# One shared gather for six rarely used neighbour slots, removed-edge cells fetched once at the end, and a payload move cut in four, in a four-layer graph kernel on one core

## The chip, the cores and the metric

The kernel runs on one core of a Trainium2 chip. A core has five engines that work side by side, each with its own queue of instructions in a fixed order: PE (matrix products), DVE (vector work), ACT (scalar functions and copies), POOL (here mostly the issue of indirect DMAs, that is gathers) and SyncE (SP, which issues plain DMAs). The metric is the device time of one execution in microseconds. Ten executions of the kernel before gave a median of 1512.22 us, from 1508.64 to 1516.35.

## The reference

Sixteen independent graphs of 1024 nodes with 64 features go through four layers. Each layer normalises the nodes, takes the positive part, does something with the adjacency matrix (0 or 1, about four neighbours per node, not symmetric) and adds the result to x. Layers 0, 1 and 3 are dense products with the adjacency matrix. Layer 2 is the one that matters here:

```python
# --- layer 2 (adj_preln) ---
h = jnp.maximum(_layernorm(x, axis=-1), 0.0)
adj_ = jnp.where(eye[None], 1.0, adj)
nb = (adj_ > 0) & (~eye)[None]              # neighbours without oneself
m = nb.sum(-1)
rank = jnp.cumsum(nb, axis=-1) - 1
skip = jnp.where(m > 10, (m + 1) // 2, 1)   # nodes of more than 10 neighbours lose some
do_dil = (skip > 1) & mask
removed = nb & do_dil[..., None] & ((rank + 1) % skip[..., None] == 0)
rem = removed | jnp.swapaxes(removed, 1, 2) # an edge is removed both ways
adj_d = jnp.where(rem, 0.0, adj_)
# per node and feature: the neighbours' h sorted, and a weighted sum of their
# quartiles (0.25, 0.5, 0.25), interpolated between ranks
agg = _weighted_nanquantile_agg(h, adj_d > 0)
y = relu((h + agg) @ W1 + b1) @ W2 + b2
x = x + y * mask[..., None]
```

So each node's few neighbours (with itself) have to be fetched as rows of h and sorted per feature.

## The kernel before

**Pairs and phases.** The graphs are worked on in eight pairs (`fast`, line 1794). For each pair, `first` loads the adjacency rows (`fast_graph`, line 1087: one 512 KB transfer of 128 rows on SyncE's queue, transposed on PE, copied by ACT, counted by ACT, the positions of the first eight neighbours found by DVE), orders the nodes by degree (`by_degree`, line 1111), makes neighbour lists (`dilated`, line 1202) and computes layers 0 and 1 and the normed input of layer 2, which goes to a table in DRAM (`fast_to_table`, line 1558). `second` gathers and sorts (`fast_quantiles`, line 1367), brings the sums back into the order of the nodes (`unsorted`, line 1467) and computes the rest of layers 2 and 3 (`fast_to_output`, line 1629). `first` of the next pair stands in the program before `second` of this one, so the two overlap.

**Sorting by degree.** The 1024 nodes of each graph are cut into 16 pieces of 64 nodes of falling degree; the two graphs of a pair lie side by side on the 128 partitions. A piece has room for only as many neighbours as its largest node needs: `CAPS = (15, 7, 6, 6, 5, 5, 5, 4, 4, 4, 3, 3, 3, 2, 2, 1)`. The lists are moved into this order by a product with one-hot matrices; for it, one DVE instruction (line 1174, `moved`) multiplies each node's payload of 11 numbers with its one-hot piece, 128 x 2816 elements.

**Lists.** The piece of the largest nodes has 16 slots: 15 for neighbours and one for the node itself. The positions of the neighbours beyond eight are found in the nodes' own adjacency rows, which POOL fetches with one gather (`high`, line 1212), then DVE runs some thirty small instructions that end in the indices `idx`, the cells of removed edges `where`, and the weights. For each pair POOL fetches from DRAM the cells that lie opposite to removed edges (`hits`, lines 1275 to 1287; two gathers). They are given a due time that is 150 us later (`LATE`).

**Gathers.** Each slot of each piece is one gather of 128 rows of 64 floats (line 1323): 75 neighbour slots and 16 own slots, so 91 per pair. The slots lie in three tiles: piece 0 (16 slots), pieces 1 to 6 (8 slots each) and pieces 7 to 15 (5 slots each). DVE sorts the three one after the other with min and max networks (`compared`, line 1328), with one scratch tile `side`.

**Buffers.** The matmul outputs of the phases have buffers of their own: `prod` and `node`, one each for the first graph's layers, the second graph's layers, and `second` (phase `_b`). All products of `second`, among them layer 3's, take turns in its single `prod`.

**The order of the work.** Nothing is issued as it is written. `Plan` (line 243) notes every instruction with a cost and a landing time from `cost` (line 380), and a due time `want` (66 us per graph, `PERIOD`). `order` (line 309) then plays the engines through: at each step an engine takes, of the instructions whose inputs are ready in the plan, the one whose due time less the longest path behind it is least. That fixes the queue of each engine; on the chip each engine waits at the head of its queue.

**The check at the end.** `checked` (line 1846) compares counts with what the lists held, and marks in `bad` and `over` the pairs for which the lists were not enough; a removed edge whose opposite cell is set also marks its pair. `redo` (line 1042) sums the marks on PE (`any_node`, line 973), and a loop of a general, slow version runs for marked graphs only. These instructions come after the plan, and their places in the queues are found by the framework: `seen` and `bad` run at 1276 to 1277 us, the last of `bad` at 1400.33 us, the sum on PE at 1400.90 us. In the time shown the loop has no turn.

## Time and profile before

| | |
|---|---|
| median of ten executions | 1512.22 us |
| profiled execution: time, span | 1510.82 us, 1509.0 us |
| busy: PE, DVE, ACT, POOL | 1054.1, 954.3, 740.6, 812.2 us |
| gathers of neighbours: count, mean | 600, 1064 ns |
| gathers of the nodes themselves: count, mean | 128, 1089 ns |
| gathers of cells (`hits`): count, mean | 16, 1035 ns |
| payload move: count, duration | 8, 3083 ns |
| TensorE clock granted, mean | 0.866 of full |

A line of the profile names the engine, the operation, the tile it writes, the tiles it reads, shapes, and how often; in an order of time the first number is the start from the beginning of the span, the second the time it took, and the brackets hold how long the engine stood idle before it and what ended that. Nearly all instructions are issued from one line of the program (369), so a step is told by its tiles: `slots` are the gathered rows, `side` the sorts' scratch, `high` the fetched adjacency rows, `prod` and `node` matmul outputs, `rest` and `low` the parts of a product's operand, `u`, `x`, `h` node features, `back` one-hot matrices. For a SyncE issue the time in an order of time that is merged runs over several, their waits included.

### The profile page before, as it was taken

The page shows a single profiled execution, that of the slowest core. Times are in us where ns is not written, and L with a number is a line of the kernel's source. Part 1 is how long each engine was busy: PE and PEld are TensorE (multiplying, and loading weights), DVE is VectorE, ACT ScalarE, POOL GpSimd, SP SyncE. Part 2 cuts the span into 40 slices and gives each one's busy share as a digit, 9 for nine tenths or more (in the row PEclk, how much of TensorE's full clock was granted, in tenths as well). Part 3 has the DMA queues.
Part 4 walks back from the last instruction along what each step waited for, and adds up shares of the span by engine and source line. Part 5 has one row for each costly group of instructions (what it writes and reads, how often), then busy time and mean ns, then how long its engine had stood idle before and what let it go on. Part 6 is the DMA issues. An engine that isn't in the chain of part 4 may idle for free.

```text
span 1509.0 us, 26159 instructions
## 1 busy us (share of the span) xinstructions
PE 1054.1 (70%) x9898; PEld 649.9 (43%) x9898; DVE 954.3 (63%) x2375; ACT 740.6 (49%) x2010; POOL 812.2 (54%) x771
## 2 busy tenths in 40 slices
PE   1588696739876879688867886797868974620266
PEld 1355463415554455445643554455544542210132
DVE  7536574877578839675868756966687467510841
ACT  1947846733565575645574557556653531210012
POOL 2000277827772778267845776277717772777000
PEclk9989797869998999899989998998989997755577
DMA  4604413512252333222343234223411111111000
GB/s 124 206 3 135 125 24 106 156 46 39 54 156 55 90 84 101 89 71 53 98 127 79 47 86 150 71 42 93 115 52 32 32 31 27 25 33 26 10 1 17
DMA packets 96111, 109.98 MB, mean 73 GB/s; under 512 B 66792, under 2 KB 66920, under 8 KB 95976
## 3 DMA queue, kind: packets, MB, share of 16 engines
q1 hardware_dynamic: 36840, 71.66, 14.9%
q0 software_dynamic: 24960, 28.11, 10.2%
q10 hardware_dynamic: 34176, 8.46, 2.6%
q8 instruction: 79, 1.29, 0.4%
q14 instruction: 56, 0.46, 0.1%
HBM read 99.77 MB, written 8.39 MB: 72 GB/s over the span
## 4 chain that ended last, share of the span: by engine, by line
POOL 51%; issue 20%; DVE 12%; PE 10%; DMA 4%; ACT 3%; SPq 0%; ACTq 0%; DVEq 0%; POOLq 0%
POOL slots L369 51%; PE prod L369 7%; DVE slots L369 3%; DVE side L369 3%; PE node L369 2%; ACT u L369 2%; DMA high<-in_adj_dram,at_row 1%; DMA slots<-table,self_idx 1%; DVE found L369 1%; ACT junk L369 1%; DMA row<-in_adj_dram 1%; DVE agg_low L369 1%; DVE more L369 1%; DVE past L369 0%; DMA slots<-table,idx 0%
## 5 line engine op out<-in xcount | busy, mean ns | idle before, releaser
L369 POOL DMA_INDIRECT slots<-table,idx x600 | 638.3, 1064 | 381.2 <-issue 208.7
L369 PE MATMUL prod<-at,rest 128*64 128x512 fp8e4 x1280 | 220.5, 413 | 90.3 <-DVE rest L369 87.3
L369 PE MATMUL prod<-at,low 128*64 128x512 fp8e4 x1280 | 218.8, 408 | 12.4 <-DVE low L369 12.0
L369 PE MATMUL prod<-at,u 128*64 128x512 fp8e4 x1280 | 218.2, 408 | 8.4 <-ACT u L369 8.0
L369 DVE TENSOR_TENSOR side<-slots 128x384 f32<-128x384 f32 (+6 forms) x160 | 92.3, 616 | 187.9 <-DMA slots<-table,self_idx 156.6
L369 ACT ACTIVATE u<-node,d 128x64 f32<-128x64 f32 x640 | 140.6, 333 | 76.2 <-PE node L369 75.7
L369 PEld LDWEIGHTS <-rest 128*64 128x64 bf16 x1792 | 99.1, 117 | 171.8 <-DVE rest L369 104.3
L369 ACT COPY rest<-prod 128x512 f32<-128x512 f32 x80 | 47.2, 591 | 256.5 <-PE prod L369 234.3
L369 ACT ACTIVATE junk<-row,unit 128x1024 fp8e4<-128x1024 f32 x128 | 150.1, 1172 | 41.7 <-DMA row<-in_adj_dram 40.8
L369 POOL DMA_INDIRECT slots<-table,self_idx x128 | 139.4, 1089 | 39.0 <-issue 38.4
L369 DVE FIND_INDEX8 found<-ones,row 128x8 uint32<-128x1032 f32 x128 | 156.5, 1224 | 0.0
L369 ACT ACTIVATE at<-tr 128x1024 fp8e4<-128x1024 bf16 x128 | 132.1, 1055 | 48.5 <-PE tr L369 30.1
L369 ACT ACTIVATE u<-x,off,by 128x64 f32<-128x64 f32 x384 | 133.8, 438 | 22.5 <-DVE off L369 18.5
L369 PEld LDWEIGHTS <-u 128*64 128x64 bf16 x1792 | 100.9, 117 | 98.7 <-issue 28.1
L369 PEld LDWEIGHTS <-low 128*64 128x64 bf16 x1792 | 99.0, 116 | 92.0 <-DVE low L369 23.2
L369 PE MATMUL tr<-ident_bf,row 128*128 128x128 bf16 x1024 | 84.5, 238 | 52.8 <-ACT at L369 52.5
L369 PE MATMUL prod<-back,side 64*64 64x512 bf16 x256 | 54.7, 402 | 77.8 <-DVE side L369 77.8
L369 PEld LDWEIGHTS <-row 128*128 128x128 bf16 x1024 | 70.6, 107 | 69.5 <-issue 65.3
L369 PE MATMUL node<-wbd,ft_sb 128*128 128x128 f32 x512 | 96.9, 290 | 4.0 <-ACT ft_sb L369 4.0
L369 DVE TENSOR_TENSOR rest<-u 128x512 f32<-128x512 f32 x80 | 54.8, 689 | 63.5 <-ACT u L369 62.9
L369 PE MATMUL node<-ident,rest 128*128 128x128 f32 x384 | 81.3, 295 | 15.2 <-ACT rest L369 15.1
L369 PEld LDWEIGHTS node<-wbd,ft_sb 128*128 128x128 f32 x512 | 78.6, 204 | 6.9 <-ACT ft_sb L369 5.0
(228 smaller groups left out, 1958.4 us busy)
## 6 DMA issues: line engine op xcount, KB each, us to landing
row<-in_adj_dram SPq DMA_DIRECT2D x128, 512.0 KB
slots<-table,idx POOLq DMA_INDIRECT x600
x<-in_x_dram ACTq DMA_DIRECT2D x32, 128.0 KB
table<-h SPq DMA_DIRECT2D x32, 128.0 KB
out_dram<-u ACTq DMA_DIRECT2D x32, 128.0 KB
slots<-table,self_idx POOLq DMA_INDIRECT x128
hits<-in_adj_dram,where POOLq DMA_INDIRECT x16
wd<-in_L_gnn_W_dram SPq DMA_DIRECT2D x2, 64.0 KB
```

Of the source, the lines that this page charges most:

```text
L369: f(*[real(x) for x in s.args], **{k: real(x) for k, x in s.kw.items()})
```

## The change

Six slots of piece 0, those for the tenth to the fifteenth neighbour, are used by few of its 64 nodes, and by the ones of highest degree, which lie first. `SHARED` gives each of these slots a number of leading nodes: 24, 12, 8, 8, 6, 6, together 64. Their indices are put below one another in one index column `rare`, by twelve small SyncE transfers from `idx` (one per slot and half); one gather fetches these 128 rows into `got`; PE moves them to their places with one matrix of shifts per slot, on top of a product that fills the places of the other nodes with a large number, and ACT copies the result into the slots (`shared`). The check of capacities now knows the number of nodes per slot.

The cells of removed edges are no longer fetched per pair. The first 16 nodes of each half write their cell numbers and flags to a common tile `cells` (two small SyncE transfers and an ACT copy per pair), and `strike`, which is noted ahead of the last pair's `second`, fetches them all with four gathers and multiplies them with the flags into `struck`. `bad` no longer reads fetched cells: it takes the flags of nodes beyond the first 16 alone; `struck` is summed on PE with two further matmuls for each half.

The payload move is issued as four instructions of a quarter each. `past` shares a buffer with `there`. The planner's costs are new on all engines, and every instruction notes a stage name, which nothing reads here.

```diff
+SHARED = ((9, 24), (10, 12), (11, 8), (12, 8), (13, 6), (14, 6))
+NEAR = SHARED[0][0]
+FIRST = 16
@@ cost
-        return 1.3, 1.7 if out.shape[-1] < N else 3.5
+        return 1.33, 1.7 if out.shape[-1] < N else 3.5
...
-            return (0.065 if narrow else 0.145), 0.2
+            return (0.067 if narrow else 0.115), 0.2
         if any(x.dtype in NARROW for x in wide):
-            return max(0.06, n * 0.25e-3), 0.25
-        return max(0.1, n * 1.15e-3), 0.25
+            return max(0.03, n * 0.213e-3), 0.25
+        return max(0.06, n * 0.9e-3), 0.25
     if engine == "scalar":
-        more = 0.19 if kw.get("accum_out") is not None else 0.0
-        return 0.19 + 0.84e-3 * n + more, 0.06
+        more = 0.2 if kw.get("accum_out") is not None else 0.0
+        for x in ("scale", "bias"):
+            more += 0.1 if isinstance(kw.get(x), Noted) else 0.0
+        return 0.18 + 0.84e-3 * n + more, 0.06
@@ sorted_constants
+        for n, (k, w) in enumerate(SHARED):
+            nc.vector.tensor_scalar(held, place, float(w), None, ALU.is_lt)
+            nc.vector.tensor_tensor(self.caps[:, 0:1], self.caps[:, 0:1], held, ALU.add)
...
+            nc.vector.memset(self.shifts[:, n, :], 0.0)
...
@@ by_degree
-        nc.vector.tensor_tensor(
-            moved,
-            pay.unsqueeze(2).to_broadcast([P, 2 * T, S, PAY]),
-            tile_hot.unsqueeze(3).to_broadcast([P, 2 * T, S, PAY]),
-            ALU.mult,
-        )
+        for a in range(0, 2 * T, HT):
+            shape = [P, HT, S, PAY]
+            nc.vector.tensor_tensor(
+                moved[:, a : a + HT],
+                pay[:, a : a + HT].unsqueeze(2).to_broadcast(shape),
+                tile_hot[:, a : a + HT].unsqueeze(3).to_broadcast(shape),
+                ALU.mult,
+            )
@@ dilated
-        self.plan.want += LATE
-        for n in range(2):
-            nc.gpsimd.indirect_dma_start(
-                out=self.hits[pair][:, n : n + 1],
...
-        self.plan.want -= LATE
+        nc.scalar.copy(cell[:, 2:4], gone)
+        for i in range(2):
+            nc.sync.dma_start(
+                out=self.cells[pair * FIRST : (pair + 1) * FIRST, i, :],
+                in_=cell[i * HP : i * HP + FIRST, :],
+            )
...
+        rare = self.p_lists.tile([P, 1], U32, name="rare")
+        off = 0
+        for k, w in SHARED:
+            for i in range(2):
+                a = i * HP
+                nc.sync.dma_start(
+                    out=rare[a + off : a + off + w, :], in_=idx[a : a + w, k // E, k % E : k % E + 1]
+                )
+            off += w
@@ new
+    def shared(self, out, table, index):
+        nc = self.nc
+        got = self.p_sort.tile([P, F], F32, name="got", bufs=1)
+        self.gather(got, table, index)
+        n = len(SHARED)
+        ps = self.ps_prod.tile([P, n, F], F32, name="rare", tag="prod")
+        nc.tensor.matmul(
+            ps,
+            lhsT=self.ident,
+            rhs=self.absent.unsqueeze(2).to_broadcast([P, n, F]),
+            start=True,
+            stop=False,
+        )
+        for k in range(n):
+            nc.tensor.matmul(
+                ps[:, k, :], lhsT=self.shifts[:, k, :], rhs=got, start=False, stop=k == n - 1
+            )
+        nc.scalar.copy(out, ps)
@@ fast_quantiles
-                for k in range(cap):
+                for k in range(NEAR if s == 0 else cap):
                     self.gather(slots[:, s - lo, k, :], table, own[:, k : k + 1])
+                if s == 0:
+                    self.shared(slots[:, 0, NEAR:cap, :], table, rare)
                 self.gather(slots[:, s - lo, cap, :], table, self_idx[:, s : s + 1])
@@ fast
             if pair + 1 < len(pairs):
                 first(pair + 1)
+            else:
+                self.strike()
             second(pair)
@@ new
+    def strike(self):
+        nc = self.nc
+        where = self.p_lists.tile([P, 2, 2], U32, name="where", bufs=1)
+        nc.vector.tensor_copy(where, self.cells[:, :, 0:2])
+        hits = self.p_lists.tile([P, 2, 2], F32, name="hits", bufs=1)
+        nc.gpsimd.memset(hits, 0.0)
...
+        for i in range(2):
+            for n in range(2):
+                nc.gpsimd.indirect_dma_start(
+                    out=hits[:, i, n : n + 1],
...
+        nc.vector.tensor_tensor(self.struck, hits, self.cells[:, :, 2:4], ALU.mult)
@@ checked
-            nc.vector.tensor_tensor(bad[:, :, S : S + 2], hits, gone, ALU.mult)
+            nc.vector.tensor_scalar(bad[:, :, S : S + 2], gone, self.spare, None, ALU.mult)
@@ redo
                 flags = self.any_node(
-                    pool, self.ps_tr, f"batches{i}", self.over, self.halves[:, i : i + 1]
+                    pool,
+                    self.ps_tr,
+                    f"batches{i}",
+                    self.over,
+                    self.halves[:, i : i + 1],
+                    [(self.struck[:, i, n : n + 1], self.pair_rows) for n in range(2)],
                 )
```

## The prediction

> **What bounds the kernel now.** I read the page's busy shares and its chain first, then the stretches cut at the ends of POOL's gather runs, then POOL, DVE and SyncE in order of time.
>
> ```profile
> PE 1054.1 (70%) x9898; PEld 649.9 (43%) x9898; DVE 954.3 (63%) x2375; ACT 740.6 (49%) x2010; POOL 812.2 (54%) x771
> POOL 51%; issue 20%; DVE 12%; PE 10%; DMA 4%; ACT 3%; SPq 0%; ACTq 0%; DVEq 0%; POOLq 0%
> ```
>
> PE is busiest, but the chain that ends last is POOL's: 51%, and most of the 20% "issue" is the 0.30 us between two gathers. The averages hide two alternating stretches, here for pair 2 (start and end; then PE, PEld, DVE, ACT, POOL):
>
> ```profile
> 484.00:611.80 127.80, 107.34 (x1039) 67.27 (x1034) 88.75 (x205) 75.27 (x214) 100.07 (x92) 0.95 0.35 88
> 611.80:646.60 34.80, 20.79 (x217) 12.63 (x214) 28.39 (x75) 19.97 (x42) 2.94 (x3) 0.85 0.27 85
> ```
>
> Some 127 us of back-to-back gathers (91 per pair), then a gap in which DVE is 82% busy and POOL waits. What ends each (POOL's order of time, then DVE's):
>
> ```profile
> 611.79 0.94 POOL L369 DMA_INDIRECT high<-in_adj_dram,at_row  x1 [0.30 <-issue]
> 646.64 1.17 POOL L369 DMA_INDIRECT slots<-table,idx  x1 [31.28 <-DVE weights L369]
> ```
>
> ```profile
> 563.05 2.76 DVE L369 TENSOR_TENSOR side<-slots 128x1152 f32<-128x1152 f32 x3 [16.84 <-DMA slots<-table,self_idx]
> 614.97 1.90 DVE L369 TENSOR_TENSOR side<-slots 128x576 f32<-128x576 f32 x3 [6.67 <-DMA slots<-table,self_idx]
> ```
>
> DVE waits 6.67 us for the last gather, so the run is POOL's. The row of the next pair's largest nodes (high) is fetched only behind the run, and the neighbour lists come out of it among the sort's own work, so the gap is DVE's. First gathers at 176.55, 328.46, 483.99, 646.64, 805.24, 967.17, 1125.67 and 1282.00 make seven periods of 157.9 us. The end is another matter (POOL, then DVE):
>
> ```profile
> 1396.74 0.94 POOL L369 DMA_INDIRECT slots<-table,self_idx  x1 [0.30 <-issue]
> 1397.98 1.01 POOL L369 DMA_INDIRECT hits<-in_adj_dram,where  x1 [0.30 <-issue]
> ```
>
> ```profile
> 1400.33 0.17 DVE L1865 TENSOR_TENSOR bad<-hits,gone 128x16 f32<-128x16 f32 x1 [69.55 <-DMA hits<-in_adj_dram,where]
> 1402.08 2.75 DVE L369 TENSOR_TENSOR side<-slots 128x1152 f32<-128x1152 f32 x3
> ...
> 1423.34 1.89 DVE L369 TENSOR_TENSOR side<-slots 128x576 f32<-128x576 f32 x3
> ```
>
> DVE stands 69.55 us before one 0.17 us instruction that needs the last fetched cell. Behind it in DVE's queue is the last pair's middle sort, whose gathers had long come; its 21.3 us fall behind the gathers instead of beside them.
>
> **The change, part by part.** The sum is made against the profiled execution: span 1509.0, time 1510.82, which is 1.40 under the median 1512.22.
>
> *Gathers.* Per pair, six gathers of slots 9 to 14 become one: 91 to 86. A run of 91 takes 126.5 us (176.55 to 303.0, and alike later), 1.39 each; the last run (1282.0 to 1398.0) 1.274 each. So 7 x 5 x 1.39 + 5 x 1.274 = 55.1 us off the path, if the other engines follow: term -55.
>
> *The middle step they leave to PE.* The shared gather's 128 rows are moved by seven float32 matmuls into PSUM and copied by ACT. PE: two 128x512 float32 matmuls took 2.07 us, so one of 384 columns 0.8; eight 128x64 took 1.06, so six 0.8; ACT's copy of 384 about 0.5 (0.59 for 512). 2 us per pair, beside the gathers. But the PSUM buffer is the single "prod" of the output phase, so these matmuls stand behind the previous pair's last product:
>
> ```profile
> 549.27 0.59 ACT L369 COPY rest<-prod 128x512 f32<-128x512 f32 x1 [0.21 <-PE prod L369]
> ```
>
> That is 65 us into pair 2's run. The first sort, which started 23 us in (506.81), has to wait until about 68; its own DVE work adds up to 15.6 us, and DVE idles 16.84 before the middle sort, so it fits, but the middle sort then starts about 568 for 563.05 and eats the 6.67 us margin at 614.97, of which the shorter run has already taken its part. The margins at that place are 2.90, 6.67, 12.84, 6.01, 11.14 and 10.50 us in the pairs 1 to 6, while 6.9 goes. Bounds 0 (the work freed at 507 is done earlier) and 5 us in each of seven periods; I take 1.4, since four of six margins are near or over what goes: +10.
>
> *The twelve index transfers.* SyncE issues twelve 4-byte-per-row transfers that build the shared index, after idx, per pair; POOL's shared gather waits for the last, and every later gather stands behind it. The planner reckons 12 x 0.08 + 2.2 us, so it puts the shared gather about fourth, 3.75 us in. SyncE's real issue time:
>
> ```profile
> 6.83 3.07 SPq L634 DMA_DIRECT2D table<-big  x4
> ```
>
> A row load's issue is 327 ns in the answer for that tile, and the four one-row writes above come 0.77 apart with waits. Landing: 2.68 us from start to landed for the gather of 451.33. So the last index lands 12 x 0.3 + 2.5 = 6.1 us after idx at the row loads' pace, 11.7 at the other. The gathers start about 0.3 us after idx, so POOL stands 0 to 8 us per pair; I take 2.0 (the row loads are the plain case): 8 x 2 = +16. The Trainium skill speaks against this part: "DMA: Bandwidth & Descriptors", section "Anatomy of one DMA", gives each DMA a fixed cost of about 2.0 us, most of it the receipt of the write. If the twelve did not overlap, its estimate would be 24 us per pair and the sum some 160 us worse; the four writes within 3.07 us say that they do overlap.
>
> *The payload move.* One DVE instruction becomes four with the same elements. Before, one gather stretches under it (DVE, then POOL):
>
> ```profile
> 538.15 3.08 DVE L369 TENSOR_TENSOR moved<-pay,tile_hot 128x2816 f16<-128x2816 f16 x1
> ```
>
> ```profile
> 538.21 3.83 POOL L369 DMA_INDIRECT slots<-table,idx  x1 [0.30 <-issue]
> ```
>
> 3.83 for 0.945, 2.5 us in the mean over seven such runs. Under three instructions in a row of 0.94 (882.67) the gather took 1.81, 0.87 over. So 0 to 2.5 us per run; I take 2.5 - 0.9, times seven, rounded: -10. On DVE the split itself costs three starts, about 0.2 us, beside gathers.
>
> *The fetched cells.* Sixteen gathers of cells go; twelve of them lie in the gap behind high or at the start (145.91), where POOL waits for the lists: nothing, while that wait lasts; without that cover, 1.3 us each. One stands ahead of the last run (1280.54, 1.46 us to the next): -1.4. Four new ones come at the end, plus two small SyncE transfers and an ACT copy per pair (0.2 us beside the lists). If the four stand behind the last gathers they cost nobody but the product with the flags; a DVE queue that puts it before the last sort would pay 4 x 1.27 = 5. I take 0, since POOL has gathers that are due sooner.
>
> *The end.* The flag instruction no longer needs a fetched cell. The middle sort goes beside the gathers, and the last sort starts at landing, 1396.74 + 2.7 = 1399.4 for 1423.34: -24.
>
> *The constants.* Some 40 small DVE instructions before the first graph. ACT's first copy waits 18.39 us for DVE's constants (34.28), so that stretch is on the path; sixteen such copies took 1.25 us, so at about 0.1 each: +4, bounds 0 to 6.
>
> *The planner's costs.* They change on every engine, so the whole order is written anew. The new ones: 0.109 us for a 512-column product matmul (0.108 measured between starts), 1.33 for a gather (1.39), but 0.33 for an ACT instruction with a column scale, which comes every 0.22. No net sign; up to 5 us per period either way, 35 in all.
>
> Sum: -55 + 10 + 16 - 10 - 1 - 24 + 4 = -60; 1510.8 - 60 + 1.4 = 1452.
>
> **The rivals.**
> 1. *DVE becomes the bound of the runs.* The late first sort pushes the middle one by the full 5 us each period, and the new order another 2: 7 x 7 = 49 for my 10, 1491. For it: margins of 2.90 and 6.01. Against: 17 us of DVE idle just where the sort goes.
> 2. *The end stays.* The new product with the fetched cells, or PE's sum of the flags, is put ahead of the middle sort or the first one's matmuls and waits for POOL: the 24 and the 5 return, 1481. For it: that is what happened to the flag before. Against: the product is now in the written order, where the sorts are due sooner.
> 3. *SyncE holds POOL up: slower.* SyncE's queue is in order, and it waits most of the time:
>
> ```profile
> SPq L369 <- PE tr L369: 641.2, 64, 59.2
> ```
>
> A row load put ahead of the index transfers makes them, POOL and all gathers wait for a transpose; the mean wait is 10 us. It decides from 2 + 60 / 8 = 9.5 us per pair; at 10 + 2, the time is 1452 + 8 x 10 = 1532. Against: in the gap of pair 3 no row load is issued between 625 and 650.66, and idx comes at 643.50.
> 4. *The lists come earlier.* If high is put among the gathers, the gap shrinks to what the table leaves (written at 643.21, gathers at 646.64) and to the sort: some 7 us in seven periods, 1403. Against: gathers that can go have stood ahead of it in seven of seven pairs.
>
> **How the numbers follow.** Forecast 0.60 (its own range 1420 to 1485), rival 1 0.13, rival 2 0.10, rival 3 0.12, rival 4 0.05. The measurement tells 0.2%, 3 us, from no change. Faster are the forecast, rivals 2 and 4 and most of rival 1: 0.85; the edge of rivals 1 and 3 within 3 us: 0.03; slower 0.12. The range reaches over rivals 1 and 2 and leaves out rival 3 and half of rival 4: 1405 to 1508.
>
> **What would show it.** Right: 86 gathers in runs of some 118 us; periods near 152; no DVE wait over 10 us in the last run; no gather over 2.5 us beside the payload move; the first sort some 65 us into a run. Wrong: a gather that waits over 5 us for a SyncE transfer; the last sort's wait for gathers gone while the period stays near 158; a DVE or PE wait of tens of us for the fetched cells at the end.

## The result, and the profile after

The changed kernel takes 1581.76 us in the median of nine executions (1570.62 to 1586.14), the kernel before 1512.43 in the median of 31: ratio 1.0457, 95% interval 1.0441 to 1.0472. It is 69 us slower where 60 us faster was forecast. The profiled execution after took 1589.87 us, its span 1588.1.

The page's busy shares and its chain of waits, after. The chain breaks off in the last stage (its shares sum to some 5%) and is of no use here.

```profile
PE 1095.3 (69%) x10018; PEld 662.5 (42%) x10018; DVE 961.2 (61%) x2443; ACT 743.9 (47%) x2026; POOL 743.4 (47%) x721
PE 3%; DVE 1%; ACT 1%; DMA 0%; issue 0%; DVEq 0%; ACTq 0%
```

POOL is busy 69 us less (52 fewer gathers at some 1.06 us make 55 of it), and the kernel is longer: POOL now waits. A run is here a pair's gathers one behind the other, a gap the time between two runs. Here are the stretches cut at the ends of gather runs, for pair 2 and for the gap behind pair 5's run (start and end; then PE, PEld, DVE, ACT, POOL):

```profile
515.02:627.80 112.78, 98.85 (x860) 59.77 (x861) 66.63 (x160) 74.39 (x202) 86.56 (x87) 0.89 0.39 109
627.80:679.51 51.71, 36.30 (x379) 20.24 (x376) 49.08 (x122) 18.94 (x54) 1.08 (x2) 0.85 0.12 27
1136.34:1228.87 92.53, 75.81 (x691) 41.96 (x689) 56.68 (x150) 42.32 (x124) 2.17 (x2) 0.89 0.14 39
```

The run is 15 us shorter (127.80 before), the gap 17 us longer (34.80 before). DVE has 66.63 us of work beside the gathers for 88.75 before, and 49.08 in the gap for 28.39: work has moved from where it was hidden to where POOL waits for it, and DVE is busy 95% of that gap. Pair 5's gap is longer still. What ends each, in order of time (POOL, SyncE, then DVE):

```profile
627.80 1.08 POOL L372 DMA_INDIRECT high<-in_adj_dram,at_row  x1 [0.30 <-issue]
679.51 1.33 POOL L372 DMA_INDIRECT got<-table,rare  x1 [50.63 <-DMA table<-h]
```

```profile
667.34 8.72 SPq L372 DMA_DIRECT2D rare<-idx  x12
676.17 0.92 SPq L372 DMA_DIRECT2D table<-h  x2
...
1225.35 0.93 SPq L372 DMA_DIRECT2D table<-h  x2
```

```profile
589.83 1.29 DVE L372 TENSOR_TENSOR side<-slots 128x512 f32<-128x512 f32 x2
611.32 2.76 DVE L372 TENSOR_TENSOR side<-slots 128x1152 f32<-128x1152 f32 x3
640.23 1.89 DVE L372 TENSOR_TENSOR side<-slots 128x576 f32<-128x576 f32 x3
642.97 1.28 DVE L372 SCALAR_TENSOR_TENSOR past<-numbers,near,high 128x1032 bf16<-128x1032 f16 x1
667.02 0.29 DVE L372 TENSOR_SCALAR idx<-near,table_at 128x136 uint32<-128x136 f32 x1
```

Three things are to be seen. The shared gather is the first of its run (in six of the eight runs), not the fourth, and comes 12.5 us after the indices (667.02 to 679.51; before, 3.1: 643.50 to 646.64). SyncE takes 8.72 us for the twelve transfers, 0.73 each, and writes the table's second half only behind them, at 676.17, though ACT had its last rows done at 669.30. And the three sorts start 75, 96 and 125 us into the run (23, 79 and 131 before): the last sort and `past`, the list chain's first step, start 12.4 and 15.2 us after `high`, where 3.2 and 5.9 were before. In pair 5's gap the table itself is late (1225.35), because the layers are.

The two parts that were meant to help did, one of them at a price. At the end DVE no longer waits for a cell behind the gathers. But the planner put the four gathers of cells into the last run, behind the third gather of rows, and they need the last pair's cells, which SyncE sends at 1378.02, behind twelve index transfers. POOL stands 8.70 us for them, and the four take 5.6 more (1381.35 to 1386.95). Most of the stand it would have had for the shared gather's index all the same, whose last transfer is issued by 1377.91. What the four cost is told by e13 below, where they stand last: its last run takes 122.26 us for 128.98 here, so 6.7 us, in a run that the last sort waits for. DVE, then POOL:

```profile
1380.39 0.17 DVE L372 CAST where<-cells 128x4 uint32<-128x4 f32 x1 [7.10 <-DMA cells<-cell]
1388.12 0.16 DVE L372 TENSOR_TENSOR struck<-hits,cells 128x4 f32<-128x4 f32 x1 [2.34 <-DMA hits<-in_adj_dram,where]
1452.29 2.76 DVE L372 TENSOR_TENSOR side<-slots 128x1152 f32<-128x1152 f32 x3
...
1499.83 1.90 DVE L372 TENSOR_TENSOR side<-slots 128x576 f32<-128x576 f32 x3 [25.13 <-DMA slots<-table,self_idx]
```

```profile
1381.35 1.01 POOL L372 DMA_INDIRECT hits<-in_adj_dram,where  x1 [8.70 <-issue]
```

Beside the payload's four instructions the longest gather of pair 2's run (POOL) takes 2.43 us (3.83 before):

```profile
583.62 2.43 POOL L372 DMA_INDIRECT slots<-table,idx  x1 [0.30 <-issue]
```

### The profile page after: what moved, and what is told of

Read it like the earlier page. It is cut to its first block, busy times and chain, and to the rows that moved or that the text cites. A ratio compares the mean times of both kernels' runs of the same rounds, so it can differ in the third digit from the quotient of the medians.

```text
span 1588.1 us, 26591 instructions
## 1 busy us (share of the span) xinstructions
PE 1095.3 (69%) x10018; PEld 662.5 (42%) x10018; DVE 961.2 (61%) x2443; ACT 743.9 (47%) x2026; POOL 743.4 (47%) x721
## 3 DMA queue, kind: packets, MB, share of 16 engines
q10 hardware_dynamic: 34176, 8.46, 2.4%
## 5 line engine op out<-in xcount | busy, mean ns | idle before, releaser
L372 POOL DMA_INDIRECT slots<-table,idx x552 | 569.5, 1032 | 216.0 <-issue 166.4
L372 PE MATMUL prod<-at,rest 128*64 128x512 fp8e4 x1280 | 235.7, 424 | 103.4 <-DVE rest L372 103.4
L372 PE MATMUL prod<-at,low 128*64 128x512 fp8e4 x1280 | 233.9, 419 | 18.2 <-DVE low L372 17.4
L372 PE MATMUL prod<-at,u 128*64 128x512 fp8e4 x1280 | 231.5, 423 | 15.0 <-ACT u L372 14.7
L372 POOL DMA_INDIRECT got<-table,rare x8 | 8.9, 1111 | 363.9 <-DMA cells<-cell 160.5
L372 POOL DMA_INDIRECT slots<-table,self_idx x128 | 141.8, 1108 | 39.0 <-issue 37.8
L372 PE MATMUL tr<-ident_bf,row 128*128 128x128 bf16 x1024 | 90.3, 244 | 80.3 <-ACT at L372 69.9
L372 PEld LDWEIGHTS <-row 128*128 128x128 bf16 x1024 | 74.7, 110 | 101.1 <-issue 84.3
L372 DVE TENSOR_TENSOR x<-x,u 128x512 f32<-128x512 f32 x32 | 21.9, 686 | 139.6 <-ACT u L372 139.6
```

The lines of the kernel that those rows point to most:

```text
L372: f(*[real(x) for x in s.args], **{k: real(x) for k, x in s.kw.items()})
```

## The experiments

Theory A: the shared gather's own work loses the time, by the transfers on SyncE and the late first sort. Theory B: the planner's new costs write a worse order. Theory C: any new order can cost tens of us, whatever is in it. The difficulty of this case is that every edit makes the planner write a new order on all engines, so that one part cannot be taken out without moving everything else. Most of the runs below therefore hold an order fixed and edit under it. On some chips the kernel before takes 1510 to 1514 us, as above, and on others 2270 us; ratios are always to the kernel before on the same chip, and differences in us between two runs hold to some 3 us, by which the medians of the kernel before differ on the first kind. The runs e1 to e4, e10 to e12, e15 and e16 fell on chips of the second kind.

### One part alone, planned anew (second kind of chip)

e1: the changed kernel without the shared gather (first four lines of the edit). e2: the changed kernel with the whole cost function of before (one line of it is shown). e3: both edits. e4 and e12: the kernel before with the new cost function.

```diff
-                for k in range(NEAR if s == 0 else cap):
+                for k in range(cap):
-                if s == 0:
-                    self.shared(slots[:, 0, NEAR:cap, :], table, rare)
...
-        return 1.33, 1.7 if out.shape[-1] < N else 3.5
+        return 1.3, 1.7 if out.shape[-1] < N else 3.5
```

> The changed kernel without the shared gather: all 15 neighbour slots of the largest piece have gathers of their own again, and the twelve index transfers, the matmuls into the prod buffer and the shift constants are gone; the cells at the end, the payload move in four and the new planner costs stay. Theory A (the shared gather itself loses the time: in the profile of the changed kernel POOL waits 160.5 us for transfers that SyncE issues behind the twelve, and the first sort starts 62 to 75 us into a run): gaps between gather runs go back to about 31 us and the time is 1512 - 24 (end) - 10 (move) - 1 (cells) + 2 (constants) = 1479, within 1465 to 1495. Theory B (the new planner costs lose it by a worse order): stays above 1550. Theory C (any new order is worth tens of us either way, whatever is in it): anywhere from 1450 to 1580, with gaps that differ from pair to pair.

> The changed kernel with the planner's costs of before; nothing else differs, so only the order of the instructions does. Theory A: the two waits of the shared gather are there whatever the order, 1560 to 1600. Theory B: back to where the forecast put it, 1450 to 1500. Theory C: more than 30 us away from 1582 on either side, with the loss in other pairs than before.

> The changed kernel without the shared gather and with the planner's costs of before, so the kernel before plus the cells at the end and the payload move in four. Theories A and B both say 1512 - 24 - 10 - 1 + 2 = 1479, within 1465 to 1495. Theory C: the cells' new instructions alone give a new order, so anywhere from 1450 to 1560.

> The kernel before with the new planner costs alone. Theory A: 1512 with at most 15 either way, the end stall of 69 us still there. Theory B: slower by about what the change lost beyond its forecast parts, 1560 to 1600. Theory C: 20 to 50 us away on either side.

> The kernel before with the new planner costs alone, on a chip where the kernel before takes 1512 (on the chip where it took 2270 this was 1.039 times as long). Theory B and C (the new costs write a worse order by themselves): 1545 to 1580. If the order is no worse: 1500 to 1525.

Measured ratios: e1 1.0457 (1.0434 to 1.0480), e2 1.0499 (1.0474 to 1.0524), e3 1.0250 (1.0233 to 1.0267), e4 1.0390 (1.0373 to 1.0408), e12 1.0385 (1.0337 to 1.0433). On such a chip every new order loses, with the shared gather or without it. But there PE stands as well, and the numbers can't be carried over. From e4, PE in order of time:

```profile
488.92 0.64 PE L369 MATMUL prod<-back,agg 64*64 64x512 bf16 x2 [8.97 <-issue]
508.35 0.64 PE L369 MATMUL prod<-back,agg 64*64 64x512 bf16 x2 [17.94 <-issue]
541.96 0.63 PE L369 MATMUL prod<-back,agg 64*64 64x512 bf16 x2 [32.11 <-issue]
```

PE stands up to 32 us with nothing to wait for that the profile shows, while POOL's gathers go on without a break. None of the theories' numbers is tested by this. The runs only warn that an order alone can cost some 4% there: e4 and e12 have the very instructions of the kernel before.

### The order held, ten transfers fewer

e5: the changed kernel's own order; all twelve index transfers are planned, and only the first two are issued.

```diff
-                    out=rare[a + off : a + off + w, :], in_=idx[a : a + w, k // E, k % E : k % E + 1]
+                    out=rare[a : a + HP, :], in_=idx[a : a + HP, k // E, k % E : k % E + 1]
                 )
+                self.plan.steps[-1].skip = k > NEAR
```

> The changed kernel in its very order, with two of the twelve index transfers per pair issued (all 64 rows of a half at once, all from slot 9; ten are left out, so the shared gather fetches rows of slot 9 for the slots 10 to 14 too and the output differs there). In the profile of the changed kernel the twelve take 8.7 to 9.5 us of SyncE's time and the table's second half is written behind them, so the gathers start 13.4 us after the indices. Theory A (SyncE's transfers hold POOL): ten fewer give back 10 x 0.75 = 7.5 us in each of the seven periods and at the start, less what the table would take anyway: 40 to 60 us, that is a ratio to the kernel before of 1.006 to 1.02 where the changed kernel had 1.046. Theory C (the order itself makes DVE and the layers late): the indices come late all the same, and in the longest gap (90 us) the table waits for the layers; 0 to 25 us, ratio 1.03 to 1.046.

Measured: 1542.95 us, ratio 1.0206 (1.0179 to 1.0234), so 39 us less than the changed kernel, just outside theory A's end. On this order ten transfers, with what queues behind them, are thus worth over half of the 69 us. But the gap of pair 5 stays, with the same end, and it is not the transfers' (POOL, e5):

```profile
1187.66 0.94 POOL L375 DMA_INDIRECT got<-table,rare  x1 [82.75 <-DMA table<-h]
```

### The gains alone, on the order of before

e6 leaves five of the six gathers out, e7 the cells, e8 splits the payload move, e9 does all three; the planner plans the kernel before, and the edit is made when the list is issued.

```diff
                     self.gather(slots[:, s - lo, k, :], table, own[:, k : k + 1])
+                    self.plan.steps[-1].skip = pair > 0 and s == 0 and k >= 10
...
                 out=self.hits[pair][:, n : n + 1],
...
+            self.plan.steps[-1].skip = True
...
+        self.plan.steps[-1].parts = parts
```

> The kernel before in its very order, with five of the six gathers of the slots 10 to 14 of the largest piece left out in the pairs 1 to 7 (those slots keep what pair 0 fetched, so the output differs); nothing takes their place. It prices the shorter run alone. Forecast's term: 7 x 5 x 1.39 = 49 us less, 1463; with the small margins of the last sort (2.90 us in pair 1, 6.67 in pair 2, the rest near or over the 6.9 that goes) some 44 us, 1468. If instead DVE bounds the runs, as rival 1 of the prediction had it: 10 to 25 us less, 1487 to 1502.

> The kernel before in its very order, with the sixteen gathers of single cells left out (the cells count as zero, which leaves the check for removed edges out), so that the flag instruction at the end waits for nothing. Forecast's terms: 24 us for the end and 1.4 for the cell gather ahead of the last run, 1487. If DVE or PE were the bound of the end anyway: under 8 us, over 1504.

> The kernel before in its very order, with the payload move issued as four instructions in the place of one. Forecast's term: 10 us less, 1502, and no gather above 2.5 us beside the move. If the stretched gather's time is covered by the last sort's wait, which ends later: 0 to 3 us, 1509 to 1512.

> The three edits together on the order of before: what the change would bring if its own new work and the new order cost nothing. Forecast: its gains without its costs, 1512 - 49 - 24 - 1 - 10 = 1428, within 1425 to 1445. If the gains overlap or DVE takes over as the bound: 1445 to 1475. Either way the distance from here to the 1582 of the changed kernel is what the shared gather's work and the order cost, less the 39 us that the ten transfers gave back.

Measured, beside 1513.28 for the kernel before: e6 1475.47 (ratio 0.9745, 0.9729 to 0.9761), e7 1498.60 (0.9903, 0.9886 to 0.9919), e8 1501.10 (0.9920, 0.9897 to 0.9944), e9 1442.25 (0.9529, 0.9513 to 0.9545). So 37.8 (44 to 49 had been expected), 14.7 and 12.2 us, 64.7 in sum and 71.0 together: the gains are real and don't get in each other's way. The end gave 14.7, not 25. DVE in e7:

```profile
1279.44 0.17 DVE L1870 TENSOR_TENSOR bad<-hits,gone 128x16 f32<-128x16 f32 x1
...
1358.31 2.76 DVE L373 TENSOR_TENSOR side<-slots 128x1152 f32<-128x1152 f32 x3 [21.39 <-DMA slots<-table,self_idx]
...
1407.04 1.89 DVE L373 TENSOR_TENSOR side<-slots 128x576 f32<-128x576 f32 x3 [27.39 <-DMA slots<-table,self_idx]
```

The stall is gone and the middle sort is beside the gathers, but now the gathers are beside the sort: the last run takes 121.96 us (1283.46 to 1405.42), with DVE busy for 49.34 of them, where it took 115.68 with DVE idle for most of it (26.40 us busy): 1.340 for 1.271 each. The other seven runs agree within 1.5 us, so the 6.3 us are what the cover costs. The last run also starts 1.46 us later than before (1283.46 for 1282.00) and not 1.4 sooner: the term for the cells didn't show.

### The whole change on the order of before

e10 and e13 are one kernel: the list is recorded once as before and once as changed; what both have keeps its old place (`keys` are the starts that the plan of before gave), what is new goes where its inputs are ready in the plan, the four gathers of cells go last (the 1e6), and among the instructions that are free to go the least key goes first.

```diff
-        for s in self.order():
+        for s in self.order() if self.keys is None else self.held():
...
+            s.key = self.keys.get(s.name)
+            if s.key is None:
+                s.key = 1e6 if s.name == "late" else 0.0
+                for a, ends in s.after:
+                    s.key = max(s.key, a.key + (a.cost + a.land if ends else 0.0))
```

> The whole change, on the order of before: the list of instructions is recorded twice, once as before and once as changed, and an instruction that both have is issued at the place that the planner gave it before, a new one as soon as what it reads is there, unless a new dependence forbids it (the four cell gathers stand last). Costs of the planner no longer matter. Start from the 1442 of the three gains on that order, less 6 for the five gathers of pair 0. Theory A (the shared gather's own work loses the time, whatever the order): its transfers (39 us) and the late first sort, above 1540. Theory C (the new order lost most of it): 1436 + 39 for the ten transfers + 2 to 5 us in each of eight pairs for the other two and their landing = 1490 to 1515, and up to 35 more where the first sort waits for the prod buffer.

> The same kernel as the one with the whole change on the order of before, for a chip on which the kernel before takes 1512. Theory A (the shared gather's own work loses the time, whatever the order): above 1540, ratio over 1.02. Theory C (the new order lost most of it): 1490 to 1515, ratio 0.985 to 1.00, with POOL's wait for the transfers (8 to 10 us per pair, as the traces of the other chip show it after one or two gathers) as the loss that stays.

Measured: e13 1522.96 us, ratio 1.0064 (1.0042 to 1.0086); e10, on the other kind of chip, 1.0130 (1.0098 to 1.0161). The same instructions as in the changed kernel, 58.8 us faster by their order alone, and still a little slower than the kernel before. Neither theory's number for these chips holds, and both have a part of the loss. The order's part is largest in pair 5's gap: 33.8 us in e13, 92.5 in the changed kernel, where the table comes late (1142.80 in e13 for 1225.35). That isn't all of it. By first gathers, pair 5's period is 49.4 us longer than in e13, but pair 6's 23.2 shorter, since behind the long gap its first sort starts 16 us into the run; the periods of the pairs 1 to 4 are 28.5 us longer, with the transfers ahead of the table's second half, and the last run 6.7, with the gathers of cells in it (in all 64 us between the two profiled executions). The part of the new work, the shared gather's above all but with the constants and the cells' transfers in it, is the distance to e9 less the five gathers of pair 0, which e9 keeps (its first run takes 125.9 us, e13's 119.6): 1522.96 - 1442.25 + 6.3 = 87 us. In e13, POOL (pair 5's gap, then the start of pair 2's run) and SyncE:

```profile
1113.11 0.95 POOL L403 DMA_INDIRECT high<-in_adj_dram,at_row  x1 [0.30 <-issue]
1146.94 1.28 POOL L403 DMA_INDIRECT slots<-table,idx  x1 [32.89 <-DVE pos L403]
```

```profile
503.56 1.29 POOL L403 DMA_INDIRECT slots<-table,idx  x1 [39.63 <-DVE pos L403]
514.58 1.07 POOL L403 DMA_INDIRECT got<-table,rare  x1 [8.46 <-PE node L403]
```

```profile
503.76 8.73 SPq L403 DMA_DIRECT2D rare<-idx  x12
```

POOL starts two gathers (one in three of the pairs), then stands 8.46 us for the last of the twelve (the releaser that is named had been done; the last transfer was issued at 512.49). Such waits add up to 62 us in seven pairs. The shared gather starts 2.1 us after that issue, which agrees with the some 2.0 us fixed cost per DMA that the Trainium skill states for a DMA of POOL's ("DMA: Bandwidth & Descriptors", "Anatomy of one DMA"), for the last of them alone: the twelve overlap, and what is paid twelve times is the issue.

### The shared gather's two waits, taken away one after the other

e15, e16 and e17 are one kernel: e13 with the shared gather 14 us later in the plan, behind the nine own gathers of its piece.

```diff
+        self.plan.mark = "later", 14.0
         self.gather(got, table, index)
+        self.plan.mark = None
```

> The whole change on the order of before as in e13 (twelve SyncE transfers, prod buffer), with one thing moved: the shared gather is issued behind the nine own gathers of its piece, some 12 us later, when the last transfer has landed. In e13 POOL waited 62 us in seven pairs and some 12 at the start for it. Theory S (POOL's wait for the transfers is the shared gather's main cost on that order): 1523 less 60 to 74, 1449 to 1463, ratio 0.96 to 0.967. Theory P (what ends late then is the first sort behind the prod buffer, 70 us into a run in e13, so the last sort and the next lists come late instead): 1480 to 1515.

> The kernel of e15 again, for a chip on which the kernel before takes 1512 (on the other kind PE stands up to 39 us at a time beside the gathers, and what ends late there is PE's). Theory S (POOL's wait for the transfers is the shared gather's main cost on the order of before): 1449 to 1463, ratio 0.96 to 0.967. Theory P (the first sort behind the prod buffer makes the last sort and the next lists late): 1480 to 1515.

> The kernel of e15 and e16 once more, for a chip on which the kernel before takes 1512. Theory S (POOL's wait for the transfers is the shared gather's main cost on the order of before): 1449 to 1463, ratio 0.96 to 0.967. Theory P (the first sort behind the prod buffer makes the last sort and the next lists late): 1480 to 1515.

Measured: e17 1500.06 us, ratio 0.9936 (0.9919 to 0.9952); e15 and e16, on the other kind of chip, 1.0345 (1.0319 to 1.0371) and 1.0362 (1.0341 to 1.0384). POOL no longer waits for the transfers, and of the 62 us only 23 come back (19 by the ratios): theory P's range. POOL, then DVE, in e17:

```profile
616.48 0.94 POOL L404 DMA_INDIRECT high<-in_adj_dram,at_row  x1 [0.30 <-issue]
659.07 0.94 POOL L404 DMA_INDIRECT slots<-table,idx  x1 [41.65 <-DVE weights L404]
671.12 1.21 POOL L404 DMA_INDIRECT got<-table,rare  x1 [0.30 <-PE node L404]
```

```profile
569.40 1.29 DVE L404 TENSOR_TENSOR side<-slots 128x512 f32<-128x512 f32 x2 [7.08 <-ACT slots L404]
584.97 2.79 DVE L404 TENSOR_TENSOR side<-slots 128x1152 f32<-128x1152 f32 x3
629.36 1.88 DVE L404 TENSOR_TENSOR side<-slots 128x576 f32<-128x576 f32 x3
```

The first sort starts 72 us into the run of 497.18, behind ACT's copy out of the `prod` buffer; the last sort starts 13 us after the last gather, and the lists come late with it.

e18 gives the rows another buffer, the one of the second graph's layers, which is free from the writing of the table until the next pair's second graph; for that, a pair's gathers (`fetch`, taken out of `second`) are recorded ahead of the next pair's first half.

```diff
+        self.phase = "_a1"
         ps = self.ps_prod.tile([P, n, F], F32, name="rare", tag="prod")
+        self.phase = "_b"
...
         for pair in pairs:
+            fetch(pair)
             if pair + 1 < len(pairs):
                 first(pair + 1)
```

> e17 with one thing more: the shared gather's rows are moved in the PSUM buffer of the second graph's layers (free from the table's writing until the next pair's second graph, some 28 us into a run) in place of the output's prod buffer, and a pair's gathers are recorded ahead of the next pair's first half so that the buffer is handed on in that order. The first sort can then start some 23 us into a run, as before, for 68 in e17. Theory P (the first sort behind the prod buffer is what e17 still pays): its periods of 159.6 us in the mean go back to those of the gains alone, 150.9, so 1500 - 7 x 8.7 = 1439, within 1430 to 1460, ratio 0.95 to 0.966. Otherwise (the lists or PE are late for another reason): 1475 to 1505.

Measured: 1456.53 us, ratio 0.9643 (0.9612 to 0.9675). DVE, then POOL, in e18:

```profile
506.57 1.27 DVE L404 TENSOR_TENSOR side<-slots 128x512 f32<-128x512 f32 x2
...
553.44 2.76 DVE L404 TENSOR_TENSOR side<-slots 128x1152 f32<-128x1152 f32 x3 [0.53 <-DMA slots<-table,self_idx]
...
607.82 1.88 DVE L404 TENSOR_TENSOR side<-slots 128x576 f32<-128x576 f32 x3
```

```profile
602.93 0.94 POOL L404 DMA_INDIRECT high<-in_adj_dram,at_row  x1 [0.30 <-DVE by L404]
638.30 0.94 POOL L404 DMA_INDIRECT slots<-table,idx  x1 [34.43 <-DVE weights L404]
```

The sorts are back at 22, 69 and 124 us into the run of 484.28, the gap is 35.4 us again, and the six periods from pair 1 on take 906.7 us (336.33 to 1243.07), as the gains alone had it in e9 (905.5). The time is inside theory P's range, 17 us above its 1439. So the wait for `prod` was worth 43.5 us (the recording order, which goes with the other buffer, is in that figure). With the order held and two places chosen otherwise, the change is 56 us faster than the kernel before; e18 is the fastest of the versions that leave nothing out.

### A miss: both waits away at once, by other means

e11 took the index out of one matmul and two DVE steps in place of the transfers, and the rows through the buffer of the first graph's layers; e14 is the same with the shared gather behind the nine and the index's matmul 3 us later in the plan.

```diff
+        nc.tensor.matmul(
+            ps, lhsT=self.places, rhs=near[:, 1, 1 : n + 1], start=True, stop=True
+        )
...
+        nc.vector.scalar_tensor_tensor(
+            pick, ps, 1.0, self.slot_hot, ALU.mult, ALU.mult, accum_out=at
+        )
+        nc.vector.tensor_scalar(rare, at, float(N), self.table_at, ALU.min, ALU.add)
...
+        self.phase = "_a0"
```

> As the run before, and the shared gather's two waits taken away by giving it other means: the shared index comes out of one matmul and two DVE instructions (no SyncE transfers), and its rows are moved in the PSUM buffer of the first graph's layers, which are done by then, in place of the output's prod buffer. Theory C: 1436 + some 2 us in each of eight pairs for the index = 1452, within 1435 to 1475, so faster than the kernel before by 3 to 5%. Theory A (the rows' way over PE and ACT or the got wait costs by itself): above 1490.

> The whole change on the order of before, with other means for the shared gather: its index comes out of one matmul and two DVE instructions in place of the twelve SyncE transfers, it is issued behind the nine own gathers of its piece, and its rows are moved in the PSUM buffer of the first graph's layers (done by then) in place of the output's prod buffer. Start from the 1523 of the change on that order: the waits of POOL for the transfers in its trace add up to 62 us in seven pairs and 12 at the start, and the first sort there starts some 70 us into a run for 20 to 25. Theory C2 (those two waits are all that the shared gather costs on that order): 1436 + 5 for the constants and 1 to 2 us per pair = 1450, within 1437 to 1470, ratio 0.95 to 0.97. Theory A2 (the rows' way over PE and ACT costs by itself, by PE or ACT being late elsewhere): 1480 to 1515.

Measured: e14 1689.83 us, ratio 1.1195 (1.1155 to 1.1236); e11, on the other kind of chip, 1.0842 (1.0811 to 1.0874). DVE in e14, then POOL:

```profile
565.20 0.15 DVE L404 SCALAR_TENSOR_TENSOR pick<-rare_at,slot_hot 128x6 f32<-128x6 f32 x1
...
594.74 0.16 DVE L404 TENSOR_SCALAR rare<-pick_at,table_at 128x1 uint32<-128x1 f32 x1
```

```profile
595.64 1.02 POOL L404 DMA_INDIRECT got<-table,rare  x1 [26.78 <-PE tr L404]
```

The last of the three small steps, 0.16 us, stands 29 us behind the second one in DVE's queue, and POOL with all later gathers stands for it. And "done by then" was wrong of the buffer: the first product of the next pair's first graph goes into it right behind ACT's copy of the rows (611.70, after 611.17), so the next layers were held as well. The time lies far outside both theories' ranges. Both faults are of placing, as far as this one pair was traced; the run says nothing of the shared gather's worth.

## Why the prediction was wrong, step by step

From before to after, by the runs: 1512.4 - 71 (gains, e9) - 6 (pair 0) + 21 (what e18 is above that) + 44 (`prod` buffer, e17 to e18) + 23 (transfers, e13 to e17) + 59 (order, e13 to after) = 1582. The forecast was 130 us short: 59 by the order, 34 by the first sort (44 for 10), 7 by the transfers (23 for 16), 17 by the rest of the new work (21 for the 4 of the constants) and 13 by the gains (77 for 90). The split depends on the sequence: in the changed order the transfers are worth more (ten of them 39), so a part of the 59 is theirs, by where that order puts them. Of the 21, 10.9 lie ahead of the first gather (190.18 in e18, 179.25 in e9), 1.3 in the six periods and 1.4 behind them; the other 7 are the distance of the two profiled executions to their medians.

- **The planner's costs, 0, at most 35.** The step that failed first. The new order cost 58.8 us with the instructions unchanged, outside the bounds; the largest piece is pair 5's gap, where the layers and so the table came late (58.7 us longer, of which its period and the next keep 26). Whether the new costs or the new instructions upset it was tried only on the other kind of chip and stays open. "No net sign" had no run behind it. That the order at hand was one that fitted, and a new one has more room on the slow side, is a guess that these runs agree with but don't show.
- **The four cell gathers, 0, at most 5.** They were taken to stand behind the last gathers, "since POOL has gathers that are due sooner". They stand in the last run, behind a wait for SyncE that the prediction didn't have, and make it 6.7 us longer than e13's, where they stand last. The 6.7 are in the order's 59.
- **First sort behind `prod`, +10.** Right mechanism, mis-sized: 43.5. That it would start about 65 us into a run was near (70 to 75 in six of the runs, 16 in the one behind the long gap). The step "the middle sort then starts about 568 for 563.05" failed: among the layers' instructions on DVE the sort took 21.5 us for its 15.6 of own work (589.83 to 611.32; some 20 before), and the middle sort began 17 us later into its run than before (96 for 79). The upper bound of 5 us per period was no bound (43.5 / 7 = 6.2). This is rival 1, whose 49 us were near, though 14 of them were meant for the order.
- **The twelve transfers, +16.** Right mechanism, wrong pace: 0.73 us each, the other end of the bracket, not the row loads' 0.3. POOL's wait for them was worth 23 us on the held order, with the first sort late all the same; ten of them 39 in the changed one. The shared gather was put first, not fourth, and the table's second half behind the twelve was not thought of. "About 0.3 us after idx" holds for two of the seven later runs before (328.46 and 483.99); the others start 0.6 to 2.9 us after it, at 646.64 because of the table (written from 643.21). Rival 3 (slower, from 9.5 us per pair) named SyncE, by another queue mate: gathers 12.5 to 13.4 us after the indices (667.02 to 679.51, 834.23 to 847.63) are past its point.
- **Gathers, -55.** The runs shrank as worked out (86 gathers in 112 to 118 us in six runs; pair 1's and the last take 129 to 130, with a wait in each). On the held order 35 of the 40 gave 37.8, so some 43 for all, by estimate. That the rest went into the last sort's wait, as the small margins said, was not traced.
- **The end, -24, and the cells, -1.4.** The stall went as forecast; 14.7 for 25, since the gathers beside DVE's sort take 6.3 us more and the run starts 1.46 later, not 1.4 sooner. Of the sixteen cell gathers fourteen, not twelve, lie in the gaps or at the start.
- **The payload move, -10.** Right: 12.2.
- **The constants, +4.** About right on the held order, where `high` for pair 0 starts at 132.23 in e18 for 128.28 in e9; 133.75 for 126.03 in the changed kernel. The first gather came 20 us later than before (196.91 for 176.55); what else is in it was not tried.

Of the signs named beforehand, "a gather that waits over 5 us for a SyncE transfer" was the one that told. The last sort's wait was gone too (640.23), but the periods didn't stay near 158, they went to 167 in the mean. The mechanisms were nearly all listed; what failed was to take the low end for two of them, and to give the order and the place of the cell gathers no price. The forecast's 1452 is near e18's 1456.5, but by luck, not by the same sum: the gains are 77 for 90, and what is left of the costs is 21 for 30.

## What to carry to other kernels

Where a planner writes the order, price a change by holding the old order and editing under it, and then price the new order by itself; here the second was 59 us, against gains of 77. A short wait put at the head of a run is paid by everything queued behind it, so place the step that waits behind work that doesn't, and look first whose buffer it takes. Small transfers cost their issue: here 0.73 us each, on the queue that the next large one needs.

## What was not expected of the hardware

- On chips of the second kind the kernel before takes 2270 us for 1512. In e4's waits there, PE's weight loads stand 791.6 us with no visible releaser (226.2 in the kernel before on the first kind), and DVE waits 665.0 for a releaser that isn't in the trace. In the stretch shown above PE stands beside an unbroken gather run. The granted clock is lower (0.718 for 0.866), but PE's busy time is only 68 us longer (1122.2 for 1054.1), so that isn't the 842 us between these two profiles:

```profile
PEld L369 <- issue: 791.6, 612, 32.6
DVE back L369 <- remote: 665.0, 38, 52.4
```

  The moves that broke or delayed POOL's gathers were not worse there: e13's kernel, with POOL's wait, had 1.013 and e17's, without it, 1.035, the reverse of their order on the other chips. The cause was not tried. The Trainium skill ("Runtime: NRT & Kernel Launch", "Instruction fetch mechanics") says that an engine fetches its instructions in blocks of 16 KiB by a DMA queue of its own, mostly hidden; one of the two instruction queues in e4's page (79 packets, 1.29 MB) agrees with the size, but the same row stands in the page of the kernel before on the first kind, and no run here shows whether PE stood for it.
- With DVE's sorts beside them the gathers of the last run take 1.340 us each, without them 1.271 (e7 and before; DVE busy 49.34 and 26.40 us).
- Twelve transfers of 4 bytes per row take 8.73 us to issue, at 6 to 24 rows each.
